# q by seven products of halves: sums on VectorE, norms on ScalarE, one image's q in the middle of round 20

## The chip, the core and the metric

The kernel runs on one core of one Trainium2 chip. The metric is the device time of a whole execution in microseconds (us). Before the change three runs took 3412.16, 3412.25 and 3413.07 us, median 3412.25. Engines are named as the profile names them: PE is TensorE (PEld its weight loads), DVE VectorE, ACT ScalarE, POOL GpSimd, SP the engine that issues most DMAs.

## What is computed

Eight images of 512 channels and 64 × 64 pixels go through two layers, in float32. The first layer is attention with deformed sampling. Cut to what matters:

```python
def _L0_conv_ref(x, w_q, w_off1, b_off1, w_off2, w_kv, w_out, b_out):
    ...
    q = jnp.einsum('oc,bchw->bohw', w_q, x)
    ...
    t = oi[:, :, ::DOWNSAMPLE, ::DOWNSAMPLE] * w_off1[None, :, None, None] + b_off1[None, :, None, None]
    t = jax.nn.gelu(t, approximate=False)
    ...
    kv_feats = grid_sample_bilinear(oi, vgrid)
    ...
    sim = jnp.einsum('bhid,bhjd->bhij', qh, kh)
    attn = jax.nn.softmax(sim, axis=-1)
    ...
x = x + _L0_conv_ref(_gn(x), ...)
x = x + _L1_conv_ref(_gn(x), ...)
```

`_gn` normalises groups of 16 channels. q is a product of a 512 × 512 matrix with 4096 pixels per image. The second layer (here: layer 1) is a small bottleneck on the first one's result.

## The kernel before, in words

**Tiles and places.** Channels lie on 128 partitions in four groups (`cc`); pixels go in eight tiles of 512 (`NT`, `TP`). Images live in two regions of SBUF, by turns, each with a spare tile beside it. `spot` (L96) lays an image out so that q tile t stands where x tile t − 1 stood (`x_tile` L101, `q_tile` L104), and the result one tile further back: q overwrites x as it goes. The weights of q, of k and of v share one buffer, `wbuf`, by turns; layer 1 also works in it.

**The q of one image.** `norm_x` (L193) takes statistics on VectorE, `group_stats` (L162) makes mean and scale per channel with two small matmuls. `project_q` (L199) then takes each tile: `normalise` (L205) on VectorE for tile 0 and on GpSimd for the others; for each of four output groups four accumulating matmuls of 128 × 128 weights with 512 columns (L252); a copy from PSUM on ScalarE (L259). A float32 matmul of the source is two instructions in the profile, so a group is eight. Between the groups stand the transposes of the tile before: `by_pixel` (L217) transposes four blocks into one PSUM bank (L226), a copy goes to a buffer `qr` (L234 on VectorE for odd steps, L236 on ScalarE for even ones), and SP stores it to `qd` in DRAM (L237), by pixel. `tensor_reduce` (L265) keeps the largest magnitude of each tile.

**Sampling.** `sample` (L279) runs gelu on ScalarE over every sixteenth pixel (L292), computes positions by small matmuls (L304), tanh (L313) and some twenty short operations on VectorE, fetches rows of `qd` by indirect DMAs from GpSimd (L396), weighs them on VectorE (L362 to L367), and turns the result into channels. `project_k` and `project_v` (L404, L431) follow.

**What sets the order.** Everything is under `manual_schedule`: each engine takes its instructions in program order, and the tile framework only adds the waits for data. After a first stretch for images 0 and 1 (L907 to L934), the loop at L935 goes through 32 rounds per image, one for each pixel tile and pair of heads. A round issues `weighted_values` (L468), for every second round `sum_exps` (L492), `add_exps` (L485) and `invert` (L511, a reciprocal on VectorE and four small DMAs on SP), then the `logits` (L449) of the next round, whose exponentials ScalarE computes (L465), and six rounds later `project_out` (L538). Four buffers `es` hold exponentials; `free_es` lists the free ones.

Beside that runs a generator, `next_image` (L860), stepped twice a round by `fill`, once ahead of `project_out` and once behind it, from round 5 or 6. It takes layer 1 of the image before, loads the next image, takes its statistics, and then `ready_q` (L899), which is `group_stats` and `project_q`, and `sample`. A `yield` of `None` ends a step; a number doesn't, up to 200, so that the whole q of an image goes in one step. In round 30 the rest is drained and `project_k` follows. In the first stretch the q of image 1 is dealt out between the steps of `sample(0)` by the numbers it yields: 4 for a group, 0.64 for a set of transposes, 7 to a step. `load_weights_late` loads `wout`, the weights of `project_out`, with other weights, behind x and the first k and v weights.

Of the kernel before, what the change touches and what calls it, by code (L numbers as in the profile page):

```python
# [8 lines left out]
F32 = mybir.dt.float32  # L9
I32 = mybir.dt.int32  # L10
AF = mybir.ActivationFunctionType
ALU = mybir.AluOpType
AX = mybir.AxisListType
# [3 lines left out]
P = 128  # L17
B = 8
C = 512
NCC = C // P  # L20
HW = 64
N = HW * HW
TP = 512
NT = N // TP
# [25 lines left out]
def kernel(  # L50
# [15 lines left out]
    nc = tc.nc  # L66
# [34 lines left out]
    def x_tile(b, t):  # L101
        return spot(b, t + 1)

    def q_tile(b, t):  # L104
        return spot(b, t)
# [20 lines left out]
    free_es = list(es4)  # L126
# [10 lines left out]
    def load_wkv(part):  # L137
        wv = w_kvT.rearrange("(cc p) o -> p cc o", p=P)
        nc.sync.dma_start(wbuf, wv[:, :, part * C : (part + 1) * C])

    def load_weights_late():
        nc.sync.dma_start(wout, w_outT.rearrange("(cc p) o -> p cc o", p=P))
        nc.sync.dma_start(convw, conv_wT.rearrange("(cc p) o -> p cc o", p=P))
        nc.sync.dma_start(outw, out_wT)
        nc.sync.dma_start(fc2b, fc2_bias)

    def col(k, n=1):
        return vec[:, k : k + n]
# [4 lines left out]
    def drain(*gens):  # L153
        for gen in gens:
            for _ in gen:
                pass


    def new_stats(which, b):
        return small.tile([P, NCC, NT, 6], F32, tag=f"st{which}", name=f"st{which}_{b}")  # L160
# [32 lines left out]
    def norm_x(b, st, order=range(NT)):  # L193
        for t in order:
            for cc in range(NCC):
                nc.vector.bn_stats(st[:, cc, t, :], x_tile(b, t)[:, cc, :])  # L196
                yield None

    def project_q(b, st, mq, qd, pools):  # L199

        gs = yield from group_stats(st, 0, b)

        qd_px = qd.rearrange("(g h p j) d -> h p g (j d)", g=HEADS, p=P, j=2)

        def normalise(t):  # L205
            xt = x_tile(b, t)
            for cc in range(NCC):
                (nc.gpsimd if t else nc.vector).tensor_scalar(  # L208
                    xt[:, cc, :],
                    xt[:, cc, :],  # L210
                    gs[:, 0, cc : cc + 1],
                    gs[:, 1, cc : cc + 1],
                    ALU.subtract,
                    ALU.mult,
                )

        def by_pixel(t, k, bank=(ps_a, "pa")):  # L217

            h, ch = divmod(k, 2)
            px = q_tile(b, t)[:, :, 2 * P * h : 2 * P * (h + 1)].rearrange(  # L220
                "p c (n j) -> p c j n", j=2
            )
            pt = bank[0].tile([P, 2, 2 * P], F32, tag=bank[1], name=f"pqt_{b}_{t}_{k}")
            for j in range(2):
                for i in range(2):
                    nc.tensor.transpose(  # L226
                        pt[:, j, i * P : (i + 1) * P], px[:, 2 * ch + i, j, :], ident
                    )
            pool, tag = pools[k % len(pools)]
            qr = pool.tile([P, C], F32, tag=tag, name=f"qr_{b}_{t}_{k}")  # L230
            qr_out = qr.rearrange("p (g j d) -> p j g d", j=2, d=DH)
            qr_in = pt.rearrange("p j (g d) -> p j g d", d=DH)
            if k % 2:
                nc.vector.tensor_copy(qr_out, qr_in)  # L234
            else:
                nc.scalar.copy(qr_out, qr_in)  # L236
            nc.sync.dma_start(  # L237
                qd_px[2 * t + h, :, 4 * ch : 4 * ch + 4, :],
                qr.rearrange("p (g m) -> p g m", g=4),
            )  # L240

        yield None
        normalise(0)
        yield None
        for t in range(NT):
            xt, qt = x_tile(b, t), q_tile(b, t)
            if t + 1 < NT:
                normalise(t + 1)
            for oc in range(NCC):
                pq = ps_mm.tile([P, TP], F32, tag="mm", name=f"pq_{b}_{t}_{oc}")  # L250
                for cc in range(NCC):
                    nc.tensor.matmul(  # L252
                        pq,
                        wbuf[:, cc, oc * P : (oc + 1) * P],
                        xt[:, cc, :],
                        start=(cc == 0),
                        stop=(cc == NCC - 1),
                    )
                nc.scalar.copy(qt[:, oc, :], pq)  # L259
                yield 4  # L260
                if t:
                    by_pixel(t - 1, oc)
                    yield 0.64
            if mq is not None:
                nc.vector.tensor_reduce(  # L265
                    mq[:, t, :], qt, axis=AX.X, op=ALU.max, apply_absolute_value=True
                )
        for q in range(NQ):
            by_pixel(NT - 1, q, ((ps_a, "pa"), (ps_mm, "mm"))[q % 2])
            yield 0.64  # L270

    def free_of(b):

# [4 lines left out]

    def sample(b, qd):  # L279

        while phase[0] == 0:
            yield None
        free, feats = free_of(b), feats_of(b)
        qs = [free[:, cc // 2, cc % 2 * NK : (cc % 2 + 1) * NK] for cc in range(NCC)]

# [569 lines left out]
    phase = [1]  # L855
# [4 lines left out]
    def next_image(b):  # L860

        n = b + 1
        if b:
            free = spot(b - 1, 0)
            first = layer1(b - 1, st1s.pop(b - 1), project_beside, free, free[:, 0:2, :])
            other, blocks = iter(()), ()
            if n < B:
                st = new_stats(0, n)
                blocks = norm_x(n, st)
                other = ready_q(n, st)  # L870


            first_load = 5
            ahead = 4
            slot = 0
            while first:
                if blocks is None and ahead:
                    next(other)
                    ahead -= 1
                if next(first, "end") == "end":  # L880
                    first = None
                if n < B:
                    if first_load <= slot < first_load + NT:
                        load_x(n, (slot - first_load,), nc.gpsimd)
                    if slot == first_load + 2 * NT:
                        load_wq()
                    if phase[0] and (slot == first_load + 3 or slot > first_load + 6):
                        for _ in range(4 if slot == first_load + 3 else 5):
                            if blocks and next(blocks, "end") == "end":
                                blocks = None  # L890
                slot += 1
                yield None
            yield from other
        if n < B:
            yield from sample(n, qds[n])

    qds = {}

    def ready_q(n, st):  # L899
        qds[n] = dpool.tile([N * HEADS, DH], F32, tag="qd", name=f"qd_{n}")  # L900
        mqs[n] = small.tile([P, NT, NCC], F32, tag=f"mq{n % 2}", name=f"mq_{n}")
        yield from project_q(n, st, mqs[n], qds[n], both_pools if n > 1 else both_pools[:1])
        if n:
            load_wkv(0)

    with tc.manual_schedule():
        load_x(0)  # L907
# [9 lines left out]
        st = new_stats(0, 0)  # L917
        drain(norm_x(0, st))

        for n, step in enumerate(ready_q(0, st)):  # L920
            if n == 3 * NCC:
                st = new_stats(0, 1)
                blocks, other = norm_x(1, st), ready_q(1, st)
            if n >= 3 * NCC and next(blocks, "end") == "end" and 13 * NCC <= n < 13 * NCC + 4:
                next(other)
        room = 0
        for step in sample(0, qds[0]):
            room += 7
            while room > 0:
                room -= next(other, 7) or 7  # L930
        project_k(0, mqs.pop(0), wkv[0])
        drain(other)
        logits(*names[0])
        project_v(0, wkv[1])  # L934
        for g in range(len(names) + LAG):  # L935
# [18 lines left out]
                sum_exps(*names[g - 1])  # L954
            if g < len(names):
                add_exps(*names[g])
            if summed:
                invert(*names[g - 1])
            if g + 1 < len(names):
                logits(*names[g + 1])  # L960
# [43 lines left out]
    with tc.If(large > 0):  # L1004
        with tc.For_i(0, B, 1) as i:
            b = "m"
            place[b], region[b] = i, 0
            qd = dpool.tile([N * HEADS, DH], F32, tag="qd", name=f"qd_{b}")
            load_wq()
            load_x(b)  # L1010
            st0, st1 = new_stats(0, b), new_stats(1, b)
            drain(norm_x(b, st0), project_q(b, st0, None, qd, both_pools), sample(b, qd))
            load_wkv(0)
            project_k(b, None)
            project_v(b)
            for t in range(NT):
                attention_max(b, t)
                for oc in range(NCC):
                    load_residual(b, t, oc)
                    project_out(b, t, oc, st1)  # L1020
            drain(layer1_last(b, st1, 1))
# [79 lines left out]
```

## Time and profile before

| What | Value |
|---|---|
| Median of three runs | 3412.25 us |
| The profiled execution | 3412.4 us |
| Its span | 3410.6 us |
| Mean granted clock of TensorE | 0.99 |
| Matmul instructions of q (L252) | 2048, 920.4 us busy |
| Matmuls of `project_out` (L544, image) | 3584, 822.9 us busy |
| Transposes of q (L226, image) | 896, 141.0 us busy |
| Normalising on GpSimd (L208) | 224, 464.8 us busy |
| Copies of q groups on ScalarE (L259, image) | 224, 131.0 us busy |

The span lacks 1.8 us of the execution's own time. In a group's line of the profile stand the source line, engine, operation, output and inputs, shapes and count; then busy time in all and mean nanoseconds of one; then how long the engine sat idle before them, and what ended most of that. A matmul's busy time [...]overlaps with the next, so what a stream of them costs is read from start to start. In the chain of waits each line is start, length, and what ran or was waited for.

### The profile page before, as it was taken

The page shows a single profiled execution, that of the slowest core. Times are in us where ns is not written, and L with a number is a line of the kernel's source. Part 1 is how long each engine was busy: PE and PEld are TensorE (multiplying, and loading weights), DVE is VectorE, ACT ScalarE, POOL GpSimd, SP SyncE. Part 2 cuts the span into 40 slices and gives each one's busy share as a digit, 9 for nine tenths or more (in the row PEclk, how much of TensorE's full clock was granted, in tenths as well). Part 3 has the DMA queues.
Part 4 walks back from the last instruction along what each step waited for, and adds up shares of the span by engine and source line. Part 5 has one row for each costly group of instructions (what it writes and reads, how often), then busy time and mean ns, then how long its engine had stood idle before and what let it go on. Part 6 is the DMA issues. An engine that isn't in the chain of part 4 may idle for free.

```text
span 3410.6 us, 42081 instructions
## 1 busy us (share of the span) xinstructions
PE 3321.9 (97%) x16660; PEld 1242.5 (36%) x16660; DVE 1895.9 (56%) x2958; ACT 1088.9 (32%) x1505; POOL 965.1 (28%) x726
## 2 busy tenths in 40 slices
PE   6999999999999999999999999999999999999996
PEld 3554323335332353324433244322443325433222
DVE  5433765752757427583375923668246682566665
ACT  1223332342333323233233423334233342333420
POOL 6181400162301713027040270302712036210201
PEclk9999999999999999999999999999999999999996
DMA  7222222662326523274333833247232572322713
GB/s 278 74 77 65 81 75 63 197 138 68 118 87 209 110 78 112 75 223 105 93 88 105 217 90 108 88 139 187 70 109 79 183 159 61 107 84 77 125 42 133
DMA packets 293183, 390.35 MB, mean 114 GB/s; under 512 B 17649, under 2 KB 157169, under 8 KB 292977
## 3 DMA queue, kind: packets, MB, share of 16 engines
q1 hardware_dynamic: 240368, 261.72, 23.9%
q0 software_dynamic: 52608, 125.86, 16.6%
q8 instruction: 132, 2.16, 0.3%
q14 instruction: 75, 0.61, 0.1%
HBM read 193.52 MB, written 192.94 MB: 113 GB/s over the span
## 4 chain that ended last, share of the span: by engine, by line
PE 88%; issue 4%; DVE 3%; DMA 2%; ACT 1%; POOL 1%; SPq 0%; ACTq 0%; POOLq 0%; DVEq 0%
PE pq L252 26%; PE pp L544 24%; PE ps L457 12%; PE pa L475 12%; PE pn L502 3%; PE pqt L226 3%; PE py L627 2%; PE pk L410 2%; PE pv L437 2%; PE po L770 2%; DMA out_dram<-spare 1%; DMA out_dram<-image 1%; DMA rn<-rn 1%; DVE wbuf L674 0%; PE po L304 0%
## 5 line engine op out<-in xcount | busy, mean ns | idle before, releaser
L252 PE MATMUL pq<-image,wbuf 128*128 128x512 f32 x2048 | 920.4, 595 | 2.5 <-DVE image L208 1.9
L544 PE MATMUL pp<-image,wout 128*64 128x512 f32 x3584 | 822.9, 601 | 8.9 <-DVE image L530 8.3
L465 ACT ACTIVATE es<-ps 128x1024 f32<-128x1024 f32 x512 | 500.9, 1023 | 264.0 <-PE ps L457 205.1
L252 PEld LDWEIGHTS pq<-image,wbuf 128*128 128x128 f32 x2048 | 374.9, 192 | 391.7 <-issue 379.8
L475 PE MATMUL pa<-es,vt 128*64 128x512 f32 x2048 | 488.2, 597 | 1.7 <-ACT es L465 1.7
L396 POOL DMA_INDIRECT g<-qd,row x256 | 271.5, 1061 | 765.8 <-PE pp L544 443.5
L208 POOL TENSOR_SCALAR image<-image,gs 128x512 f32<-128x512 f32 x224 | 464.8, 2652 | 0.4
L234 DVE COPY qr<-pqt 128x512 f32<-128x512 f32 x128 | 88.4, 691 | 639.5 <-PE pqt L226 634.2
L457 PE MATMUL ps<-image,kt 64*64 64x512 f32 x3584 | 437.9, 602 | 3.9 <-ACT spare L797 3.5
L544 PEld LDWEIGHTS pp<-image,wout 128*64 128x64 f32 x3584 | 237.1, 137 | 551.7 <-issue 462.6
L551 DVE SCALAR_TENSOR_TENSOR image<-pp,vec,image 128x512 f32<-128x512 f32 x224 | 167.3, 747 | 435.8 <-PE pp L544 435.0
L487 DVE TENSOR_TENSOR es<-es,es 128x1024 f32<-128x1024 f32 x256 | 310.6, 1213 | 71.4 <-PE pa L475 71.4
L259 ACT COPY image<-pq 128x512 f32<-128x512 f32 x224 | 131.0, 585 | 684.7 <-PE pq L252 684.7
L482 ACT COPY image<-pa 128x512 f32<-128x512 f32 x224 | 131.4, 586 | 673.5 <-PE pa L475 673.5
L183 POOL TENSOR_TENSOR gs<-ve,nhalf 128x4 f32<-128x4 f32 x16 | 18.0, 1123 | 1014.0 <-DVE ve L182 1014.0
L475 PEld LDWEIGHTS pa<-es,vt 128*64 128x64 f32 x2048 | 137.4, 137 | 297.4 <-issue 276.8
L457 PEld LDWEIGHTS ps<-image,kt 64*64 64x64 f32 x3584 | 114.1, 132 | 315.3 <-issue 178.7
L515 DVE RECIPROCAL rn<-pn 128x512 f32<-128x512 f32 x64 | 214.7, 3355 | 10.1 <-PE pn L502 5.9
L807 POOL DMA_DIRECT2D out_dram<-spare x56 | 68.0, 1214 | 488.1 <-ACT spare L797 469.5
L528 DVE STREAM_SHUFFLE rb<-rn 128x512 f32<-128x512 f32 x256 | 186.8, 730 | 0.1
L226 PEld LDWEIGHTS pqt<-ident,image 128*128 128x128 f32 x896 | 138.0, 203 | 100.9 <-issue 89.2
L196 DVE BATCH_NORM_STATS2 st<-image 128x6 f32<-128x512 f32 x256 | 157.4, 677 | 7.4 <-DMA image<-in_x_dram 7.2
(149 smaller groups left out, 2493.8 us busy)
## 6 DMA issues: line engine op xcount, KB each, us to landing
qd<-qr SPq DMA_DIRECT2D x256, 256.0 KB
image<-in_x_dram SPq DMA_DIRECT2D x112, 512.0 KB
out_dram<-image SPq DMA_DIRECT2D x49, 1024.0 KB
image<-in_x_dram POOLq DMA_DIRECT2D x48, 1024.0 KB, 15.2
out_dram<-spare POOLq DMA_DIRECT2D x56, 512.0 KB, 6.2
out_dram<-part POOLq DMA_DIRECT2D x112, 256.0 KB, 7.8
image<-in_x_dram SPq DMA_DIRECT2D x16, 1024.0 KB
wbuf<-in_w_kvT_dram SPq DMA_DIRECT2D x14, 1024.0 KB
```

Of the source, the lines that this page charges most:

```text
L208: (nc.gpsimd if t else nc.vector).tensor_scalar(xt[:, cc, :], xt[:, cc, :], gs[:, 0, cc : cc + 1], gs[:, 1, cc : cc + 1], ALU.subtract, AL ...
L226: nc.tensor.transpose(pt[:, j, i * P : (i + 1) * P], px[:, 2 * ch + i, j, :], ident)
L252: nc.tensor.matmul(pq, wbuf[:, cc, oc * P : (oc + 1) * P], xt[:, cc, :], start=(cc == 0), stop=(cc == NCC - 1),)
L396: nc.gpsimd.indirect_dma_start(held[-1][:, i, :, :].rearrange("p j d -> p (j d)"), None, qd[:, :], bass.IndirectOffsetOnAxis(ap=row[:, ky, ...
L457: nc.tensor.matmul(ps[k : k + DH, a, :], kt[r : r + DH, hp, kc * P + k : kc * P + k + DH], qt[r : r + DH, hp, :], start=True, stop=True,)
L465: nc.scalar.activation(e, ps, AF.Exp)
L475: nc.tensor.matmul(pa[a * DH : (a + 1) * DH, :], vt[:, kc, hd * DH : (hd + 1) * DH], es[kc][:, a, :], start=(kc == 0), stop=(kc == 1),)
L487: nc.vector.tensor_add(es[0], es[0], es[1])
L515: nc.vector.reciprocal(rn, denominators.pop((b, t)))
L528: nc.vector.stream_shuffle(rb, rn, [2 * (hp % 2) + hp // 2] * 32)
L544: nc.tensor.matmul(pp[r : r + DH, :], wout[:, hp, oc * P + r : oc * P + r + DH], ao[:, hp, :], start=(hp == 0), stop=(hp == NCC - 1),)
L551: nc.vector.scalar_tensor_tensor(xt[:, oc, :], pp, col(V_BOUT + oc), xt[:, oc, :], ALU.add, ALU.add)
```

## The change

`project_q` is rewritten. A tile of x, the weights and the tile of q are each cut in halves both ways (`quarters`): for x and q two channel groups by 256 pixels, for the weights two input groups by 256 outputs. q is then made from seven products of quarters in place of eight, by Winograd's form of Strassen's method. The products need sums of quarters of x and of the weights beforehand (`of_tile`, `of_weights`), some written in place, and additions of products afterwards (`V.tensor_add`), all on VectorE. A product is four matmuls of the source with 256 columns into one PSUM bank. The sums of the weights are made once per load of `wbuf`; image 1 uses those of image 0. The five extra arrays `sums` lie in `wout` and `kt` for images 0 and 1, and in three `es` buffers for the others.

Normalising moves to `norm_q`: tile 0 on VectorE and tile 1 on GpSimd ahead, tiles 2 to 7 on ScalarE inside, two tiles in advance (`pixels`). Copies of transposes are ScalarE's for all tiles but the last, VectorE's there. `make_q` runs in the middle of round 20, ahead of the logits, in one piece; `invert` of that round is issued behind its third tile, and the first step of `sample` (gelu) ahead of the last tile's transposes. `next_image` waits until `sample` is there. In the first stretch all of image 1's q is issued before `project_k(0)`, and `wout` is loaded behind it. In the loop for large logits at the end, which these inputs don't enter, the calls change likewise.

```diff
     def load_weights_late():
-        nc.sync.dma_start(wout, w_outT.rearrange("(cc p) o -> p cc o", p=P))
...
+    def load_wout():
+        nc.sync.dma_start(wout, w_outT.rearrange("(cc p) o -> p cc o", p=P))
...
+    def quarters(a):
+        h = C // 2
+        return [[a[:, 2 * i : 2 * i + 2, h * j : h * (j + 1)] for j in range(2)] for i in range(2)]
+    def norm_q(b, st, norms):
         gs = yield from group_stats(st, 0, b)
+        shift = small.tile([P, NCC], F32, tag="shift", name=f"shift_{b}")
+        def normalise(t, cc):
+            xc, scale = x_tile(b, t)[:, cc, :], gs[:, 1, cc : cc + 1]
+            if t < 2:
+                (nc.vector, nc.gpsimd)[t].tensor_scalar(
+                    xc, xc, gs[:, 0, cc : cc + 1], scale, ALU.subtract, ALU.mult
+                )
+            else:
+                nc.scalar.activation(
+                    xc, xc, AF.Identity, bias=shift[:, cc : cc + 1], scale=scale
+                )
+        norms[b] = normalise
+        yield None
+        for t in (1, 0):
+            for cc in range(NCC):
+                normalise(t, cc)
+        nc.vector.scalar_tensor_tensor(shift, gs[:, 0], -1.0, gs[:, 1], ALU.mult, ALU.mult)
+        yield None
+    def project_q(b, normalise, mq, qd, pools, sums, aside=None, behind=None):
...
+        s1, s2, s4, t1, t2_ = sums
+        (w11, w21), (w12, w22) = quarters(wbuf)
+        V = nc.vector
+        def of_weights(n):
+            if b == 1:
+                return
+            if n == 1:
+                V.tensor_add(s1, w21, w22)
+            elif n == 2:
+                V.tensor_sub(s2, s1, w11)
+            elif n == 3:
+                V.tensor_sub(w21, w11, w21)
+            else:
+                V.tensor_sub(s4, w12, s2)
+        def of_tile(t, n):
+            (x11, x12), (x21, x22) = quarters(x_tile(b, t))
+            if n == 1:
+                V.tensor_sub(t1, x12, x11)
+            elif n == 2:
+                V.tensor_sub(t2_, x22, t1)
+            elif n == 3:
+                V.tensor_sub(x12, x22, x12)
+            else:
+                V.tensor_sub(x21, x21, t2_)
+        def product(bank, w, xh):
+            for o in range(2):
+                for k in range(2):
+                    nc.tensor.matmul(
+                        bank[:, o * 2 * P : (o + 1) * 2 * P],
+                        w[:, k, o * P : (o + 1) * P],
+                        xh[:, k, :],
+                        start=(k == 0),
+                        stop=(k == 1),
+                    )
+            return bank.rearrange("p (o n) -> p o n", o=2)
...
+        def one_bank(t, n):
+            return ps_mm.tile([P, TP], F32, tag="mm", name=f"pq_{b}_{t}_{n}")
+        def two_banks(t, n):
+            two = ps_s.tile([P, 2, TP], F32, tag="s", name=f"pq_{b}_{t}_{n}")
+            return two[:, 0, :], two[:, 1, :]
...
             qr_in = pt.rearrange("p j (g d) -> p j g d", d=DH)
-            if k % 2:
+            if t == NT - 1:
                 nc.vector.tensor_copy(qr_out, qr_in)
             else:
                 nc.scalar.copy(qr_out, qr_in)
...
-        yield None
-        normalise(0)
-        yield None
+        for n in range(1, 4):
+            of_weights(n)
+            of_tile(0, n)
         for t in range(NT):
-            xt, qt = x_tile(b, t), q_tile(b, t)
+            (x11, x12), (x21, x22) = quarters(x_tile(b, t))
+            (q11, q12), (q21, q22) = quarters(q_tile(b, t))
+            def pixels(k):
+                if t:
+                    by_pixel(t - 1, k)
+                if t + 2 < NT:
+                    normalise(t + 2, k)
+            bank1, bank2 = two_banks(t, 0)
+            nc.scalar.copy(q11, product(bank1, w11, x11))
+            yield 2
+            p6 = product(one_bank(t, 1), s2, t2_)
+            pixels(0)
+            V.tensor_add(q12, q11, p6)
+            yield 2.5
+            p2 = product(bank2, w12, x21)
+            V.tensor_add(q11, q11, p2)
+            of_tile(t, 4)
+            if t == 0:
+                of_weights(4)
+            yield 2
+            p7 = product(one_bank(t, 2), w21, x12)
+            pixels(1)
+            V.tensor_add(q22, q12, p7)
+            yield 2.5
+            bank1, bank2 = two_banks(t, 3)
+            p5 = product(bank1, s1, t1)
+            pixels(2)
+            V.tensor_add(q12, q12, p5)
             if t + 1 < NT:
-                normalise(t + 1)
-            for oc in range(NCC):
-                pq = ps_mm.tile([P, TP], F32, tag="mm", name=f"pq_{b}_{t}_{oc}")
-                for cc in range(NCC):
-                    nc.tensor.matmul(
-                        pq,
-                        wbuf[:, cc, oc * P : (oc + 1) * P],
-                        xt[:, cc, :],
-                        start=(cc == 0),
-                        stop=(cc == NCC - 1),
-                    )
-                nc.scalar.copy(qt[:, oc, :], pq)
-                yield 4
-                if t:
-                    by_pixel(t - 1, oc)
-                    yield 0.64
-            if mq is not None:
...
+                of_tile(t + 1, 1)
+                of_tile(t + 1, 2)
+            yield 2.5
+            p4 = product(bank2, w22, x21)
+            pixels(3)
+            V.tensor_add(q21, q22, p4)
+            V.tensor_add(q22, q22, p5)
+            if t + 1 < NT:
+                of_tile(t + 1, 3)
+            yield 2.5
+            p3 = product(one_bank(t, 4), s4, x22)
+            V.tensor_add(q12, q12, p3)
+            if t + 1 < NT:
+                largest(t)
+            if t == 2 and aside:
+                aside()
+            yield 2
+        if behind:
+            behind()
         for q in range(NQ):
             by_pixel(NT - 1, q, ((ps_a, "pa"), (ps_mm, "mm"))[q % 2])
             yield 0.64
+        largest(NT - 1)
...
-        while phase[0] == 0:
-            yield None
...
-                other = ready_q(n, st)
+                other = norm_q(n, st, norms)
...
-            yield from other
+            if n < B:
+                drain(other)
+                while n not in samples:
+                    yield None
         if n < B:
-            yield from sample(n, qds[n])
+            yield from samples[n]
...
+    Q_ROUND = 20
+    def make_q(n, sums, aside=None):
+        pools = both_pools if n > 1 else both_pools[:1]
+        samples[n] = sample(n, qds[n])
+        yield from project_q(
+            n, norms[n], mqs[n], qds[n], pools, sums, aside, lambda: next(samples[n])
+        )
         if n:
             load_wkv(0)
...
+    def room_for_sums(tiles):
+        return [
+            tiles[i // 2][:, i % 2, :].rearrange("p (k o) -> p k o", k=2) for i in range(5)
+        ]
...
-        for n, step in enumerate(ready_q(0, st)):
-            if n == 3 * NCC:
-                st = new_stats(0, 1)
-                blocks, other = norm_x(1, st), ready_q(1, st)
-            if n >= 3 * NCC and next(blocks, "end") == "end" and 13 * NCC <= n < 13 * NCC + 4:
-                next(other)
+        shared = [wout[:, i, :].rearrange("p (k o) -> p k o", k=2) for i in range(3)]
+        shared += [kt[:, 0:2, :], kt[:, 2:4, :]]
+        drain(norm_q(0, st, norms))
+        st = new_stats(0, 1)
+        blocks, other = norm_x(1, st), norm_q(1, st, norms)
+        for n, step in enumerate(make_q(0, shared)):
+            if n >= 3 * NCC and next(blocks, "end") == "end" and n >= 10 * NCC:
+                next(other, None)
+        drain(other)
+        other = make_q(1, shared)
         room = 0
-        for step in sample(0, qds[0]):
-            room += 7
+        for step in samples[0]:
+            room += 6
             while room > 0:
-                room -= next(other, 7) or 7
+                room -= next(other, 6) or 6
+        drain(other)
+        load_wout()
         project_k(0, mqs.pop(0), wkv[0])
-        drain(other)
...
+            if r == Q_ROUND and 0 < b < B - 1:
+                tiles = [free_es.pop(0) for _ in range(3)]
+                drain(make_q(b + 1, room_for_sums(tiles), lambda: invert(*names[g - 1])))
+                free_es.extend(tiles)
+            elif summed:
                 invert(*names[g - 1])
```

## The prediction

> **What bounds the kernel now.** I read the page's busy shares and clock first, then the chain of work through one image's q, then ScalarE's timeline for the price of a matmul, then the groups.
>
> ```profile
> span 3410.6 us, 42081 instructions
> PE 3321.9 (97%) x16660; PEld 1242.5 (36%) x16660; DVE 1895.9 (56%) x2958; ACT 1088.9 (32%) x1505; POOL 965.1 (28%) x726
> PEclk9999999999999999999999999999999999999996
> PE 88%; issue 4%; DVE 3%; DMA 2%; ACT 1%; POOL 1%; SPq 0%; ACTq 0%; POOLq 0%; DVEq 0%
> ```
>
> TensorE is the bound, at nearly full clock throughout; VectorE has 44% of the span free, ScalarE 68%. The chain through the q of image 2:
>
> ```profile
> 732.33 17.36 PE pq L252 x40
> 749.69 0.46 PE pqt L226 x4
> 750.16 3.44 PE pq L252 x8
> ...
> 855.08 0.48 PE pqt L226 x4
> ...
> 856.19 2.27 DVE mq L265
> ```
>
> TensorE does nothing but q for 126.8 us: 32 groups of eight matmul instructions at 3.434 us (109.9), 28 sets of four transposes at 0.47 (13.1), and from 855.56 to 859.12, where the next projection begins, 3.56 us for the last four sets, which wait for copies behind the reduction on VectorE. Images 3 to 7 have the same stretch (1147.9 to 1274.7, 2810.2 to 2937.0). The price of a matmul stands in ScalarE's timeline, which copies each group as it ends; above 512 columns, below 256:
>
> ```profile
> 42.21 0.58 ACT L259 COPY spare<-pq 128x512 f32<-128x512 f32 x1 [2.85 <-PE pq L252]
> 45.65 0.58 ACT L259 COPY spare<-pq 128x512 f32<-128x512 f32 x1 [2.85 <-PE pq L252]
> ...
> 540.29 0.38 ACT L417 ACTIVATE kt<-pk 128x256 f32<-128x256 f32 x1 [1.34 <-PE pk L410]
> 542.02 0.38 ACT L417 ACTIVATE kt<-pk 128x256 f32<-128x256 f32 x1 [1.34 <-PE pk L410]
> ```
>
> Eight instructions take 3.434 us at 512 columns and 1.727 us at 256, with new weights for each: half the columns cost half, and the weight loads (190 ns) stay hidden. Prices on the other engines:
>
> ```profile
> L530 DVE TENSOR_TENSOR image<-image,rb 128x512 f32<-128x512 f32 x224 | 155.1, 692 | 7.8
> L551 DVE SCALAR_TENSOR_TENSOR image<-pp,vec,image 128x512 f32<-128x512 f32 x224 | 167.3, 747 | 435.8 <-PE pp L544 435.0
> L265 DVE TENSOR_REDUCE mq<-image 128x4 f32<-128x2048 f32 x56 | 127.4, 2275 | 0.0
> L802 ACT ACTIVATE part<-po,vec 128x512 f32<-128x512 f32 x112 | 70.4, 684 | 0.0
> ```
>
> **What the Trainium skill says.** "TensorE: Matmul & The Clock Gate", section "Wait — 56ns, not 53.3ns?", gives about 2.5 ns per matmul beside its columns, so that halves should cost little; the trace agrees: 429.2 and 215.9 ns an instruction, 2.6 ns more than half. "VectorE: DVE Perf Modes", "Mode 2×_2P — use both read ports for one tensor": an fp32 tensor_tensor stays at one element a cycle; 692 ns for 512 elements agrees. "SBUF — State Buffer", "SBUF: two separate sides": an operation with two SBUF inputs and a GpSimd one that reads SBUF exclude each other; the trace doesn't show it for additions, and where both engines normalise (33 to 36 us), VectorE's four took 0.68 each against 0.48 elsewhere, no full block. "ScalarE: Activation LUTs", "What ACT_TABLE_LOAD costs": 1283 ns a switch; the trace has 1283, and no drain behind it.
>
> **The change, part by part.**
>
> *Products.* A tile goes from 4 groups at 3.434 (13.74 us) to 7 products of eight 256-column instructions at 1.727 (12.09): 1.65 less, times 64 tiles 105.6 us. The transposes keep number and price (1.88 a tile), so a tile takes 13.97 in place of 15.62.
>
> *Sums on VectorE.* Per tile four sums of quarters (0.69) and seven additions from PSUM (0.69 to 0.75, I take 0.72) and the reduction (2.28): 10.1 us in 13.97. The order within a tile, from its start: product 1 ends at 1.73, 6 at 3.45, 2 at 5.65, 7 at 7.4, 5 at 9.6, 4 at 11.8, 3 at 14.0. With 0.2 us for a signal, VectorE ends the last addition of the tile before at 0.9 and its reduction at 3.2, and follows each product within 1.6 us. The tightest wait is product 4 for x21: ready at 7.2, wanted at 10.05, 2.8 us of slack; product 6 of the next tile has 3.8, product 7 has over 5. PSUM banks come free sooner still. In the steady state I charge nothing, and none of these waits can cost less than that, since the products already run at their price; if that cover were gone, each microsecond a tile costs 64.
>
> *Start of a burst.* Product 6 needs s1, t1, s2 and t2: four sums of 0.69 after add_exps, 0.35 us behind product 1's start, so product 6 starts at 3.35 and not at 1.73: 1.6 us lost per image. Bounds 0 and 3 (were GpSimd still normalising).
>
> *Normalising and copies.* GpSimd's 28 operations become ScalarE's: per tile 4 at 0.68, 4 copies from transposes at 0.59 and the first quarter at 0.59 make 5.7 us of 13.97, two tiles ahead: nothing. GpSimd's four for tile 1 (9.2 us) now stand before the last accumulating stores of layer 1; nothing of layer 1 is queued behind those, and their buffers are wanted by the q stores over 20 us later: nothing (up to 5 us otherwise). Transposes ahead of additions change no engine's order, only what can be waited for.
>
> *End of a burst.* The reduction goes behind the copies: last transposes 2.9 us instead of 3.56. But the position matmuls (L304) now come one logits step (1.9) after them, so 4.8 after the last product, and need gelu: 0.95 for the last addition, 4.2 for eight gelus, 0 to 1.3 for the table: 5.3 to 6.5. Loss 0.5 to 1.8, taken 1.1. Exponentials of the next round end 9.7 after the last product, wanted near 12: hidden.
>
> *Moves.* The burst goes from round 19 behind the logits to round 20 ahead of them. Sampling still has two steps a round up to round 30, where project_k wants it; the position matmuls stood in round 20 before too (867 us). invert goes inside: 3.36 us on VectorE, caught up within a tile (x21 at 8.7 against 10.05), and four rn transfers on SP, behind which q stores wait; with four qr buffers, each wanted a tile later: nothing. load_wout (1 MB) goes to SP behind the last product of image 1 and load_wkv, ahead of the first residual loads, and is wanted six rounds of some 9 us later: nothing, 5 us if not.
>
> *Images 2 to 7:* 1.6 + 96.7 + 13.1 + 2.9 + 1.1 = 115.4 against 126.8, 11.4 less, six times: 68.
>
> *Images 0 and 1* (263.4 us from 33.6 to 297) save 26.4, and give back: start of image 0, where all sums follow VectorE's normalising (product 6 at 38.9 us; the first group loses 1.5 there today), 2.1 (0 to 5 with GpSimd in the way); image 0 carries image 1's 32 bn_stats, 0.65 each, seven a tile: 14.7 us on VectorE, some 1 a tile over TensorE for 4.5 tiles, of which slack takes half: 2.5 (0 to 6); group_stats waits behind that queue: 1; position matmuls right after the last transposes, wanting gelu: 2 (0 to 4); the chain of some 20 small position operations (0.2 each, 4.4 us) ahead of sums: 2 (0 to 4); qr with two buffers, landing 2.4 us after the copy, wanted after 4.4: nothing. Sum given back 9.6, net 16.8.
>
> Total 68 + 16.8 = 84. The profiled execution took 3412.4 (span 3410.6 and 1.8 around it), the median is 3412.25: **3328 us**.
>
> **Rivals.**
> *The full gain:* start and end waits vanish: 3412.4 − 105.6 = 3307. Against it: s1 to t2 can't be earlier than add_exps.
> *VectorE falls behind:* additions wait in its queue behind the reduction, bn_stats or sampling, and product 4 or 6 with them, 0.5 us a tile: 32 lost, 3360. For it: before, q needed VectorE for copies only, now every product; it decides once the lag passes 2.8 us. Against: 10.1 of 13.97.
> *Slower: each product is tied to the addition before it.* q(t) is written into the image that holds x. If dependencies were kept by the span of a quarter's rows and not its exact elements, products 7, 3 and the next 1 would wait for additions into the same rows: 0.9, 1.1 and 0.9 us, 2.9 a tile against 1.65 gained: 64 × 1.25 = 80 more, 3492. It decides from 1.65 us a tile of exposed waits, 0.24 a product. Against it, from the timeline:
>
> ```profile
> 861.41 1.08 SPq L557 DMA_DIRECT2D out_dram<-image  x1
> ...
> 864.65 0.56 ACT L482 COPY image<-pa 128x512 f32<-128x512 f32 x1
> ```
>
> This 1 MB store reads four rows of an image region, interleaved with its other tiles; by the traffic per microsecond some 1.9 MB of it and of the 1 MB weight load ahead of it move only after 864.65, so most of it is still to come when ScalarE writes another tile of that region without a wait. Dependencies are kept by exact elements there.
>
> **How the numbers follow.** The forecast (3312 to 3345) has 0.60, the full gain 0.06, the lag (3345 to 3392) 0.25, the tie 0.07, no difference 0.02. Range 3307, all exposed terms nought, to 3368, the upper bounds of the start, end and first-image terms (some 25 and 15 us); most of the lag case lies inside. Within 0.2%, about what a measurement can tell from no change, is 3405 to 3419. Faster 0.91, same 0.02, slower 0.07.
>
> **What the new profile would show.** Groups of products eight at 1.73 us; a burst of about 115 us starting behind pn in round 20; 1.6 us of idle before the second product, released by VectorE's t2; about 1 us before the position matmuls, released by gelu; GpSimd's normalising down to 32 operations. Wrong if TensorE idles inside later tiles with VectorE as the releaser, or if eight products take more than 1.75.

## The result, and the profile after

Five runs of the changed kernel took 3392.08 to 3400.18 us, median **3395.13 us**, against 3412.25 before: a ratio of 0.9954 (with its 95% interval: [0.9939, 0.9968]), 17 us less. The forecast was 3328 us with a range of 3307 to 3368. The sign is right; four fifths of the 84 us are missing. The profiled execution took 3395.13 us too. Of all executions below, one of run 6 with 7482.74 us was disturbed and stands in no ratio.

The page of the kernel after, its head and the chain that ended last:

```profile
span 3393.4 us, 45885 instructions
PE 3236.2 (95%) x18196; PEld 1536.7 (45%) x18196; DVE 2313.0 (68%) x3602; ACT 1177.4 (35%) x1599; POOL 581.1 (17%) x534
PE 77%; issue 10%; DVE 5%; DMA 4%; POOL 2%; ACT 1%; SPq 0%; POOLq 0%; DVEq 0%; ACTq 0%
```

TensorE's busy time fell by 86 us, the span only by 17: TensorE now idles inside the stretch that it had filled. Its share of the chain fell from 88% to 77%, and VectorE's rose. What TensorE waits for, by line, in the list of waits (total, times, longest):

```profile
PE pq L270 <- DVE image L355: 39.8, 56, 0.8
PE ps L564 <- ACT spare L904: 13.1, 13, 2.2
PE pq L270 <- DVE spare L355: 8.7, 8, 3.2
```

The first and third are one wait, 64 times, once in each tile of each image: a product (L270) waits for `V.tensor_add(q12, q12, p5)`, L355. The third line is tile 0 of each image, whose q lies in the spare and where no transposes run. The second stood in the list before with 3.5 us. TensorE's timeline in two tiles of image 2, tile 1 above and a later one below (start, length, then in brackets the idle time ahead and its releaser):

```profile
760.48 0.63 PE L305 MATMUL pqt<-ident,spare 128*128 128x128 f32 x4
761.42 1.99 PE L270 MATMUL pq<-image,wbuf 128*128 128x256 f32 x8 [0.31 <-DVE image L355]
...
804.59 1.89 PE L270 MATMUL pq<-es,es 128*128 128x256 f32 x8
806.32 0.63 PE L305 MATMUL pqt<-ident,image 128*128 128x128 f32 x4
807.72 1.99 PE L270 MATMUL pq<-image,wbuf 128*128 128x256 f32 x8 [0.78 <-DVE image L355]
809.55 0.63 PE L305 MATMUL pqt<-ident,image 128*128 128x128 f32 x4
```

In the later tile product 5 runs from 804.59, the third transposes from 806.32 for 0.47 us, and product 4 could begin at 806.79. It begins at 807.72, 0.93 us late, and takes 1.83 us to the next start where others take 1.73: 1.03 us lost. In tile 1 it begins 0.47 late, with the same 0.10; in tile 0 it loses as much as in a later tile (product 5 from 744.68, product 4 from 747.35, the next from 749.18). So 56 × 1.03 + 8 × 0.57 = 62 us over all tiles, most of the missing 67. VectorE's timeline, for the same two tiles, has the addition that is waited for:

```profile
760.68 0.69 DVE L355 TENSOR_TENSOR image<-image,pq 128x512 f32<-128x512 f32 x1 [1.51 <-PE pq L270]
...
806.98 0.69 DVE L355 TENSOR_TENSOR image<-image,pq 128x512 f32<-128x512 f32 x1 [1.51 <-PE pqt L305]
```

VectorE is not behind: it idled 1.51 us ahead of L355. In tile 1 the addition starts 0.2 us after product 5 ended (760.48). In the later tile it starts 0.2 us after the *transposes* ended (806.79), 0.47 later, though it needs nothing from them. Tile 1 differs in one thing: its transposes read the tile of q that lies in the spare, all later ones read the image's own region, into which L355 writes. The profile's account of line L355, over the whole execution, has what ended VectorE's idle time ahead of it (total, times):

```profile
  PE pqt L305: 69.9, 48
  PE pq L270: 17.8, 15
```

The 48 are as many as tiles 2 to 7 of eight images; tiles 0 and 1 make 16.

**Theory A**, in two parts. (1) Products 5 and 4 go to the two halves of one PSUM tile (`two_banks`). The framework keeps that tile as one thing: TensorE's first write to the second bank waits for VectorE's read of the first, in every tile. (2) In a region each of the four channel groups is a row, with all pixel tiles one behind the other. The transposes issued ahead read rows 0 and 1 of one tile, L355 writes rows 0 and 1 of the next. No element is shared, but their spans overlap (everything from the first to the last element that an instruction touches); so the addition waits for the transposes.

**Rivals**: B, VectorE is the late one, and 1 us of lag shows wherever a product first needs it; C, the queue of GpSimd takes the rest; D, product 4 waits because of what the additions write into q, and the pair of banks has no part in it.

### The profile page after: what moved, and what is told of

Its sections match the earlier page's. It is cut to its first block, busy times and chain, and to the rows that moved or that the text cites. A ratio compares the mean times of both kernels' runs of the same rounds, so it can differ in the third digit from the quotient of the medians.

```text
span 3393.4 us, 45885 instructions
## 1 busy us (share of the span) xinstructions
PE 3236.2 (95%) x18196; PEld 1536.7 (45%) x18196; DVE 2313.0 (68%) x3602; ACT 1177.4 (35%) x1599; POOL 581.1 (17%) x534
## 3 DMA queue, kind: packets, MB, share of 16 engines
q0 software_dynamic: 52608, 125.86, 16.8%
## 4 chain that ended last, share of the span: by engine, by line
PE 77%; issue 10%; DVE 5%; DMA 4%; POOL 2%; ACT 1%; SPq 0%; POOLq 0%; DVEq 0%; ACTq 0%
PE pq L270 21%; PE pp L651 21%; PE ps L564 11%; PE pa L582 10%; PE pqt L305 3%; PE pn L609 3%; DMA out_dram<-image 3%; POOL out_dram L914 2%; PE py L734 2%; PE pk L517 2%; PE pv L544 2%; DMA out_dram<-spare 1%; DVE image L355 1%; PE po L877 1%; DVE mq L281 1%
## 5 line engine op out<-in xcount | busy, mean ns | idle before, releaser
L270 PE MATMUL pq<-image,wbuf 128*128 128x256 f32 x2048 | 485.8, 386 | 50.5 <-DVE image L355 39.8
L564 PE MATMUL ps<-image,kt 64*64 64x512 f32 x3584 | 439.6, 603 | 14.1 <-ACT spare L904 13.1
L270 PEld LDWEIGHTS pq<-image,wbuf 128*128 128x128 f32 x2048 | 382.5, 192 | 117.0 <-DVE image L355 50.4
L315 ACT COPY qr<-pqt 128x512 f32<-128x512 f32 x224 | 131.3, 586 | 439.8 <-PE pqt L305 250.0
L270 PE MATMUL pq<-es,es 128*128 128x256 f32 x768 | 182.1, 380 | 3.9 <-DVE es L261 3.9
L198 DVE BATCH_NORM_STATS2 st<-image 128x6 f32<-128x512 f32 x256 | 158.7, 678 | 7.6 <-DMA image<-in_x_dram 7.5
L661 DVE BATCH_NORM_STATS2 st<-image 128x6 f32<-128x512 f32 x224 | 155.6, 694 | 7.7
L637 DVE TENSOR_TENSOR image<-image,rb 128x512 f32<-128x512 f32 x224 | 155.0, 692 | 7.8
L305 PE MATMUL pqt<-ident,image 128*128 128x128 f32 x896 | 145.4, 284 | 14.7 <-DVE image L265 6.1
```

What stands on the lines that cost most here:

```text
L270: nc.tensor.matmul(bank[:, o * 2 * P : (o + 1) * 2 * P], w[:, k, o * P : (o + 1) * P], xh[:, k, :], start=(k == 0), stop=(k == 1),)
L305: nc.tensor.transpose(pt[:, j, i * P : (i + 1) * P], px[:, 2 * ch + i, j, :], ident)
L564: nc.tensor.matmul(ps[k : k + DH, a, :], kt[r : r + DH, hp, kc * P + k : kc * P + k + DH], qt[r : r + DH, hp, :], start=True, stop=True,)
```

## The experiments

The runs were made on several chips. On those of the first four the kernel before took 3434.51 us, on those of the next three 3431.61, of the last two 3408.61, so ratios to before on the same chip are compared; "on the scale of 3412" multiplies one by 3412.25.

**1. Product 4 in a PSUM tile of its own.** A bank of the ring `ps_mm` in place of the second half of the pair:

```diff
-            p4 = product(bank2, w22, x21)
+            p4 = product(one_bank(t, 5), w22, x21)
```

> Product 4 gets a PSUM tile of its own in place of the second bank of product 5's tile; nothing else changes. Theory A (product 4 waits for the addition that reads product 5, because both stand in one PSUM tile): the 1.03 us of idle per tile go, a tile takes 13.97 us in place of 15.0, 64 tiles give 66 us, 3329 us. Rival B (VectorE is late with x21 and product 4 waits for that): the wait stays, 3395 us.

Measured: 0.9756 [0.9743, 0.977], 3329 on the scale of 3412. TensorE's timeline in this kernel, around product 4:

```profile
816.13 1.89 PE L270 MATMUL pq<-es,es 128*128 128x256 f32 x8
817.87 0.63 PE L305 MATMUL pqt<-ident,image 128*128 128x128 f32 x4
818.33 1.89 PE L270 MATMUL pq<-image,wbuf 128*128 128x256 f32 x8
```

Product 4 starts as the transposes end, with no bracket: no wait. VectorE has the same work in the same order, and its addition still waits for the transposes:

```profile
818.53 0.69 DVE L355 TENSOR_TENSOR image<-image,pq 128x512 f32<-128x512 f32 x1 [1.51 <-PE pqt L305]
```

But nobody waits for it now. Rival B falls: nothing was taken off VectorE. Product 4 even starts 0.2 us ahead of this addition, though it reads x21 from rows 2 and 3 of the region in which the addition writes rows 0 and 1: sharing a region is not yet a tie. A steady tile, from first product to first product, takes 13.97 us here (751.14 to 765.11), as the prediction had it, and 15.01 in the change (796.74 to 811.75).

**2. The third transposes ahead of product 5**, the pair left as it was:

```diff
-            p5 = product(bank1, s1, t1)
             pixels(2)
+            p5 = product(bank1, s1, t1)
             V.tensor_add(q12, q12, p5)
```

> The third set of transposes of each tile is issued ahead of product 5 and not behind it. Theory A with its second half (the addition of product 5 starts only when the transposes issued between have ended, since it writes into the same image as they read): the addition starts 0.47 us earlier in the six tiles per image whose transposes read the image's region, and product 4 with it: 48 x 0.47 = 23 us less, 3372 us. If the addition follows product 5 alone, as the prediction had it, or if x21 is what product 4 waits for: 3395 us.

Measured: 1.0127 [1.0111, 1.0142], slower than the change itself, which neither side expected. The list of waits of this kernel:

```profile
PE pq L270 <- DVE image L355: 42.0, 54, 0.8
PE pqt L305 <- ACT qr L315: 37.7, 54, 0.7
```

The second and third transposes now stand back to back, and there is one PSUM buffer for them (`ps_a` with one of tag "pa"): the third waits for ScalarE's copy of the second, 54 times. A tile takes 16.01 us (818.27 to 834.28), 1.00 more than in the change: 54 of the 59 us that lie between the two ratios. That had been overlooked, and it makes the time no test. VectorE's addition and TensorE's product 4 in this kernel:

```profile
813.50 0.69 DVE L355 TENSOR_TENSOR image<-image,pq 128x512 f32<-128x512 f32 x1 [2.50 <-PE pq L270]
814.24 1.99 PE L270 MATMUL pq<-image,wbuf 128*128 128x256 f32 x8 [0.78 <-DVE image L355]
```

Product 5 ends at 813.30. L355 starts 0.2 us later, released by `pq` and not by `pqt`, and product 4 waits for it even so: both parts of theory A are seen apart from each other. The expected 23 us were not there to win in any case. From product 5's end to product 4 are now 0.94 us in place of 1.40, but the 0.47 us of transposes that filled part of the 1.40 now stand ahead of product 5.

**3. Additions ahead of transposes.** Each `pixels(k)` moved behind the additions of its product, for example

```diff
-            pixels(2)
             V.tensor_add(q12, q12, p5)
+            pixels(2)
```

> All transposes are issued behind the additions of their step instead of ahead. If waits for data are kept by the exact elements, as the prediction said, transposes and additions don't touch each other and nothing changes: 3395 us. If they are kept by the span of a quarter's rows, the transposes of the tile before wait for the additions into the next one: about 1.0 us for the first and second set, nothing more for the third, 1.7 for the fourth, in 48 tiles: 178 us more, 3573 us.

Measured: 1.0505 [1.0486, 1.0525], 3585 on the scale of 3412. What the transposes (L305) now wait for:

```profile
PE pqt L305 <- DVE image L362: 66.9, 48, 1.4
PE pqt L305 <- DVE image L339: 55.4, 48, 3.3
PE pqt L305 <- DVE image L354: 32.2, 48, 0.7
PE pqt L305 <- DVE image L349: 32.2, 47, 1.1
```

Transposes read q of tile t − 1, these additions write q of tile t: no element is shared. Still all four sets wait, 48 times each (one line has 47), which is six tiles of eight images, those whose transposes read the image's region. How they wait shows what is tied; TensorE's timeline of the first set of tile 2 in image 2:

```profile
822.00 0.27 PE L305 MATMUL pqt<-ident,image 128*128 128x128 f32 x1
823.01 0.63 PE L305 MATMUL pqt<-ident,image 128*128 128x128 f32 x3 [0.74 <-DVE image L339]
```

The first of the four transposes goes ahead; the second waits, and the others behind it. The first reads row 0, the second row 1. L339 writes rows 0 and 1 one pixel tile further on, so its span begins behind what the first transpose reads, and holds what the second reads. The other three sets of this tile divide in the same way (826.93, 830.06, 833.20). So q tiles in one region are tied by span, not by whole rows or the whole region, and the issue order of the change is what keeps this tie on VectorE's side.

A tile takes 18.51 us (818.54 to 837.05) in place of 15.01: 168 us over 48. The wait for L339, up to 3.3 us where `invert` is ahead on VectorE, has 20 us beyond 48 × 0.74. Together that is the 188 us between 1.0505 and 0.9954.

**4. As 1, and tile 1 normalised on VectorE.** A test of rival C, that GpSimd's four operations hold up its stores, and through them `ps`:

```diff
-                (nc.vector, nc.gpsimd)[t].tensor_scalar(
+                (nc.vector, nc.vector)[t].tensor_scalar(
```

> As the first run (product 4 in its own PSUM tile), and tile 1 normalised on VectorE instead of GpSimd. Theory: GpSimd's 9 us in round 18 delay the accumulating stores of layer 1 behind them, ScalarE waits for the buffer and TensorE for ScalarE, 13.1 us in all over six images against 3.5 before the change: 6 to 10 us less than the first run, 3321 us. Rival: that wait comes from the DMAs' own time and not from GpSimd's queue: as the first run, within 2 us.

Measured: 0.9776 [0.9762, 0.9789], no better than 1. The wait of `ps` for L904 is 14.9 us in place of 12.6. Taking tile 1 off GpSimd wins nothing, and rival C falls.

**5. A second pair tied.** Product 1 to a bank of its own, and products 6 and 2, between which an addition stands, into one two-bank tile:

```diff
-            bank1, bank2 = two_banks(t, 0)
-            nc.scalar.copy(q11, product(bank1, w11, x11))
+            nc.scalar.copy(q11, product(one_bank(t, 0), w11, x11))
             yield 2
-            p6 = product(one_bank(t, 1), s2, t2_)
+            bank1, bank2 = two_banks(t, 1)
+            p6 = product(bank1, s2, t2_)
```

> The version after, with a second pair of products in one two-bank PSUM tile whose second member comes straight behind an addition: product 1 goes to a bank of its own, products 6 and 2 share a two-bank tile. Theory A (TensorE's first matmul into the second bank waits for VectorE's read of the first bank, because the two-bank tile is kept as one thing): product 2 now waits for the addition of product 6 as product 4 does for that of product 5, 0.93 us of idle and 0.1 of a slower first matmul in seven tiles of an image, half the idle in tile 1: 7.8 us an image, 62 in all; 3395 + 62 = 3457 us on the scale of the first chip, a ratio to before of 1.013. Rival D (product 4 alone waits, because of what the additions write into q, and the extra bank helped by loosening the ring of banks): 3395, ratio 0.995.

Measured: 1.0213 [1.0193, 1.0234]; the change itself, beside it, had 0.9946 [0.9933, 0.996]. The difference of 0.0267 is 91 us. Waits of this kernel, and below them the timeline of TensorE and VectorE at tile 3 of image 2:

```profile
PE pq L270 <- DVE image L340: 66.4, 56, 3.2
PE pq L270 <- DVE image L355: 38.3, 54, 0.8
```

```profile
810.77 3.35 DVE L622 RECIPROCAL rn<-pn 128x512 f32<-128x512 f32 x1
814.03 0.63 DVE L340 TENSOR_TENSOR image<-image,pq 128x512 f32<-128x512 f32 x1
...
814.72 5.41 PE L270 MATMUL pq<-image,wbuf 128*128 128x256 f32 x16 [3.19 <-DVE image L340]
```

The wait appears where it was put, and the old one stays: rival D falls. It is larger than expected by nearly half (91 us against 62), partly because this addition stands behind others on VectorE: in tile 3 the reciprocal of `invert` (3.35 us) is ahead of it, so that product 2 waits 3.19 us and not 0.85, some 14 us over the six images 2 to 7. A tie costs the length of the queue in front of the tied instruction, not the instruction alone. Of the other 15 us no cause was sought.

**6. Product 2 ahead of product 6**, each in its own PSUM tile, on top of 1:

```diff
+            p2 = product(two_banks(t, 6)[0], w12, x21)
             yield 2
             p6 = product(one_bank(t, 1), s2, t2_)
...
-            p2 = product(bank2, w12, x21)
```

> The version with product 4 in its own bank, and product 2, which needs no sums, issued ahead of product 6, each in a PSUM tile of its own; the additions keep their order. Theory: the 0.9 us that product 6 waits at the start of each image for s1, t1, s2 and t2 lies behind product 2 then, 8 x 0.9 = 7 us, and transposes come one product later, so that some of the waits of transposes for VectorE (about 13 us) go: 3329 - 7 to 15 = 3314 to 3322 us on the scale of the first chip, ratio 0.971 to 0.9735. Rival: the additions of products 6 and 2 now follow each other directly, product 7 or a later one waits for them, and nothing is won: 3329, ratio 0.9756. Both must show product 6 starting 3.5 us behind product 1 with no idle.

Measured: 0.9818 [0.9804, 0.9832], slower than 1 by 0.6%, and than its repeat (run 9) by 0.4%. The wait of product 6 at the start is down to 0.4 us in all, but another has come:

```profile
PE pqt L305 <- DVE image L265: 25.2, 48, 1.7
```

Transposes now follow later, at a moment when VectorE is about to write x21 (L265) into the region they read: the tie by span again, 48 times. In 1 this wait had 7.3 us.

**7. The change unchanged**, for the ratio used above.

> The version after, unchanged, beside the others on one chip, so that their ratios have one basis. Every theory expects a ratio to before of 0.994 to 0.997.

Measured: 0.9946 [0.9933, 0.996].

**8 and 9. Product 2 ahead in tile 0 only**, where no transposes run (`if t == 0:` on the new line of 6, `if t:` on the old one, products 5 and 1 as in 1); and 1 again beside it.

> The version with product 4 in its own bank, and product 2 ahead of product 6 in tile 0 only, where no transposes run; the other tiles keep their order. Theory: product 6 no longer waits 0.9 us for the four sums at the start of an image, and the waits of transposes for the sum written into x21 (25 us, 48 times, when product 2 was ahead in every tile) stay away: 8 x 0.9 = 7 us less than with product 4 in its own bank alone, ratio to before 0.9735 against 0.9756. Rival: the order in tile 0 only shifts the wait, to product 7 or 4 behind additions that come later: no gain, 0.9756, with the 25 us still absent.

> The version with product 4 in its own bank again, unchanged, to stand beside the run with product 2 ahead in tile 0 on the same chip: ratio 0.974 to 0.977 by every theory.

Measured: 0.9745 [0.9732, 0.9759] and 0.9776 [0.9763, 0.979]. Medians of 3319.98 and 3332.07 us on one chip: 12 us less, 7 expected. The wait for L261 is down to 0.4 us, and that for L265 stays at 7.3 us. The intervals just part, so the sign is safe and the size is not. Runs 1 and 9 are one kernel and differ by 0.0020, some 7 us; with runs of the change at 0.9954 and 0.9946, parting the pair won 58 to 68 us, and the 62 of the timeline lie within. This is the best version found, 2.5% under the kernel before and 2.1% under the change.

## Why the prediction failed, step by step

*What bounds, and the price of products: right.* Eight 256-column matmuls follow each other at 1.73 us, and the four transposes at 0.47. One slip: 215.9 ns is 1.3 more than half of 429.2; the 2.6 is what two halves cost more than a whole, and that is what stands beside the 2.5 that the prediction quotes for each matmul.

*The steady state: the step that failed.* The prediction put it so: "PSUM banks come free sooner still. In the steady state I charge nothing". Banks did come free in time, but product 4's bank was not free to the framework while its neighbour in the two-bank tile was unread. The term charged at 0 is 62 us by the timeline. "Transposes ahead of additions change no engine's order, only what can be waited for" has the second half of the cause in it and doesn't price it: the addition came to wait for the transposes, so that 0.47 us, half of the 0.93, is theirs. The sign that the prediction had named for being wrong came true: TensorE idled inside later tiles with VectorE as the releaser, 64 times. VectorE was named without being late. The slack table was made of data only (which sum wants which product), and product 4 was the tightest entry for x21, with 2.8 us. The wait that ended last wasn't a data wait at all.

The two pages of the Trainium skill that bear on this agree with the runs. "PSUM — Partial Sum Buffer", section "PSUM bank collisions raise a hardware error", has engines kept apart by bank; different banks run clean. So the wait between two banks was not needed by the chip, and run 1, which takes two banks without it, shows that. "Perfetto Trace Analysis", section "Matmuls", advises rotating through different PSUM banks; here two banks weren't enough, the tiles had to be two, for 1.03 us a tile.

*The tie as a rival: right in kind, rejected on a reading that didn't reach it.* "Dependencies are kept by exact elements there" rested on one store and one copy before the change. For quarters of tiles, run 3 shows ties by span. Why that store and that copy were not tied was not tried, and stays open: by the loop's indices the copy writes row 0 of a tile behind the stored one, within the store's span. The rival as priced, 2.9 us a tile in three places, also didn't happen: the order of issue kept those ties off TensorE, and one wait of 1.03 us stayed under the 1.65 at which the change turns slower. Run 3 with its additions first is that rival come true, 5% slower.

*VectorE lagging: wrong.* It was given 0.25; VectorE idles before most additions, and run 1 wins 67 us with all its work in place. That 3395 lies just above this rival's 3345 to 3392 says nothing for it; the prediction had named no case between 3392 and 3405. The lag shows in one place: behind `invert`, which was to be caught up at no cost, transposes wait 1.01 us for the sum written into x21 (L265), 6.1 us in six images.

*Start of a burst: right in kind.* 1.6 us was charged for product 6; it starts 0.9 late, released by L261.

*End of a burst: right in sum.* TensorE's timeline of the kernel after, last product, next logits, and the position matmuls:

```profile
855.06 1.89 PE L270 MATMUL pq<-image,es 128*128 128x256 f32 x8
...
860.35 1.95 PE L564 MATMUL ps<-image,kt 64*64 64x512 f32 x16
862.23 1.95 PE L411 MATMUL po<-vec,image 128*128 128x4 f32 x16
```

From the product's end at 856.79 to the logits are 3.56 us, the same as before, not 2.9; the position matmuls then wait for nothing, where 1.1 was charged. 3.6 against 4.0. On the table load, the Trainium skill's page "ScalarE: Activation LUTs", section "What ACT_TABLE_LOAD costs", has 1283 ns for the load alone and some 2.66 us for a whole switch with its drain, where the prediction says 1283 a switch; in the trace of before the first gelu starts 0.01 us after the load's end (860.51), and the copy ahead of it ended 0.03 us before the load.

*The burst and the rest, with the pair parted: right.* The burst was forecast at 115.4 us. In the change it is 123.6 (736.75 to 860.35); with product 4 in its own bank, in run 9:

```profile
719.22 1.99 PE L270 MATMUL pq<-image,wbuf 128*128 128x256 f32 x8
...
834.93 1.95 PE L564 MATMUL ps<-image,kt 64*64 64x512 f32 x16
```

115.7. From the `pk` of image 1 to that of image 7, the mean from one to the next is 415.3 us before, 413.3 in the change and 404.8 in run 9: 10.5 less, of 11.4 forecast. Up to the first `pk` after the first stretch the change wins 0.5 us, run 9 18.0, forecast 16.8. So the other terms of the sum hold within a few us together. That is partly luck: in each of these bursts the start and the end were charged 1.1 us too much, and the 1.01 behind `invert` was not charged. Twice measured, the parted version comes to 3329 and 3336 on the scale of 3412, and 3328 was forecast for the change. ScalarE's normalising was put at 0.68 and took 0.814, 0.5 us a tile more, and stayed hidden. GpSimd's four normalisings (8.95 us in image 2) and the moves of loads cost nothing that shows.

*The range.* Its upper end was said to hold some 40 us of upper bounds. As far as the terms show them, start and end have 12.6 in six images and the first images 10.4, 33 with the two terms of 5 us; the tie of 62 stood in none of them.

*Not foreseen, and open:* the wait of `ps` for L904 grew from 3.5 to 13.1 us. L904 waits for the store of `spare` to DRAM. It is there in runs 1, 4, 8 and 9 as well (12.6, 14.9, 12.7, 12.7), so neither the pair of banks nor GpSimd's normalising makes it; where it comes from wasn't tried.

## What to carry to other kernels

Before charging nothing for buffers that come free in time, list which instructions share a tile, PSUM tiles of several banks above all, and ask for each whether the writer of one part must wait for the reader of another; what shares only a region of memory may be tied the same way. Work issued ahead to fill an engine can become what the other engine waits for: price an addition from the end of what was issued ahead, not from the end of its own product. And where a sum of gains says 84 and the clock 17, divide the rest by the number of tiles first: 67 over 64 is one wait, and the list of waits names it.

## What the runs showed of the hardware

The first eight matmuls after a wait for another engine took 0.10 us more, start to start, than eight in a stream (1.83 against 1.73). ScalarE's normalising with scale and bias per partition took 814 ns for 512 columns (L218), its activation with a bias alone from PSUM 685 (L909). At the start of image 0, GpSimd's four normalisings beside VectorE's sums took 10.57 us, and one of these sums 1.09 us where others take 0.69; in image 2 the same four took 8.95.
